# Attention with latent projections on one core: probabilities transposed and moved inside SBUF in one transfer, the division by the softmax sums put after the values, and two 64-row matmuls beside each other

## The chip, the cores and the metric

The kernel runs on one core of a Trainium2 chip. The metric is the device time of one execution in microseconds (us). Three executions of the kernel before took 1964.89, 1964.98 and 1975.46 us; the median is 1964.98 us.

Engines are named as the profile names them: PE is the matrix engine (PEld its weight loads), DVE the vector engine, ACT the scalar engine, POOL GpSimd, SP the engine that issues most DMAs. SBUF is the on-chip memory with 128 partitions, PSUM the matmul's result memory, DRAM the chip's large memory.

## The reference

```python
cq = rms_norm(x @ w_qa.T, q_a_ln_w)                       # x: 2048 x 512
q_nope, q_pe = split((cq @ w_qb.T), 128, 64)              # 16 heads
ckv = x @ w_kva.T                                         # 128 latent + 64 rotary columns
k_nope, v = split(rms_norm(ckv[..., :128], kv_a_ln_w) @ w_kvb.T)
scores = (q_nope @ k_nope.T + rope(q_pe) @ rope(k_pe).T) * 192 ** -0.5
attn = softmax(causal(scores))                            # 16 x 2048 x 2048
x = layernorm(x + (attn @ v) @ w_o.T)
x = layernorm(x + x @ (weight * scale_weight).T + bias)
```

The kernel keeps keys and values in the latent form of 128 columns (`w_kvb` is folded into the query weights and into `w_o`), so one set of keys `Kn`, `Kp` and values `V` serves all heads. Float32 accuracy is made of two parts: a number is stored as a rounded part and a rest, and a product is three matmuls (part by part, part by rest, rest by part).

## The kernel before

The 2048 queries are cut into four blocks b of 512, the 16 heads into eight pairs p. Within a block the loop `units` (L659) runs over the pairs, over four tiles qt of 128 queries, and over the two heads j of the pair. One such step, a **unit**, handles 128 queries of one head against nk = (4b + qt + 1) * 128 keys: 640 to 1024 keys in block 1, 1152 to 1536 in block 2, 1664 to 2048 in block 3. In block 0 (nk up to 512) both heads are one step. A unit has one PSUM tile of up to 1024 scores (two chunks of at most 512) where nk is at most 1024, and two tiles above.

A unit goes through these lines:

1. `score` (L421, matmuls at L431): for each chunk of keys five matmuls with 128 rows each: the query's latent part against both parts of `Kn`, its rest against the first, and two with `Kp`. In `pe`, rows 0 to 63 hold the rotary query's rounded part and rows 64 to 127 its rest; in `Kp`, rows 64 to 127 repeat rows 0 to 63. The first of the two products with `Kp` so adds (part + rest) by the key's part; the second adds (part + rest) by the key's rest.
2. DVE takes the maximum (L472) and makes the bias (L479 or L481); ACT takes the exponent into `pr` with the row's sum beside it (L487).
3. DVE makes `inv`, 16384 divided by the sum, in two small instructions (L497 or L499, and L500).
4. ACT writes `pr * inv` as float16 into the even halves of the 32-bit words of `hl` (L525), DVE the rest into the odd halves (L528).
5. `turn` (L503): DVE transposes the words in blocks of 32 x 32 (L506), back into `pr`, and SP sends the head's turned words to a DRAM tile `sq` (L509).
6. After the second head `gather` (L511) fetches both heads from `sq` into a slot of the SBUF tile `ring`, with four DMAs of 32 destination partitions each (L514). A DMA of SP waits in SP's queue, and all that is queued behind it waits too.
7. Two or three query tiles later `values` (L573, matmuls at L584) multiplies `V` with the slot. The result `ot` (L589) goes to `ot_d` in DRAM.

`pr` has 5, 3 and 2 buffers in blocks 1, 2 and 3, `hl` 4, 3 and 2; each holds a whole head. `room` (L739) gives out the slots of `ring` and runs values early where none is free. Projections of the next pair (L359, L403) are put between the units by `fill`. The order of PE and SP is as written in blocks 1 to 3, and that of DVE and ACT too from the second query tile of block 3; elsewhere a scheduler sets it.

After block 3 comes the **tail**: for 32 combinations of block and pair `latent_load` (L756) fetches `ot_d`, `latent_split` (L760) makes part and rest on ACT (L64) and DVE (L65), `accumulate` (L803) multiplies with the output weights; then the layer norms and the last matrix.

Of the kernel before, what the change touches and what calls it, by code (L numbers as in the profile page):

```python
# [49 lines left out]
def mla_block(ctx: ExitStack, tc: tile.TileContext, a, out):  # L50
# [23 lines left out]
    ot_d = [[dram.tile([P, 4, 256], F32, name=f"ot_d{b}_{p}") for p in range(NPAIR)] for b in range(NB)]  # L74

# [228 lines left out]
    later = []  # L304

# [41 lines left out]
    def project_pe(b, g, direct=None):  # L347
# [72 lines left out]

    def score(ps, c0, w, b, p, j, qt, masked):  # L421
# [14 lines left out]
        if by_product:  # L436
# [3 lines left out]
            mask()  # L440

# [3 lines left out]
    def head_scores(pools, b, p, j, qt, nk, prev):  # L445
# [6 lines left out]
        for ti, ck in enumerate(cks):  # L452
# [13 lines left out]
            for ci, (c0, w) in enumerate(ck):  # L466
# [17 lines left out]
        pr = pools[1].tile([P, nk], F32, tag="pr", name=f"pr{b}_{p}_{qt}_{j}", bufs=(5, 3, 2)[b - 1])  # L484
        sums = small.tile([P, 2], F32, tag="sums", name="sums")
        for ti, (v, c0, n, w) in enumerate(tiles):
            nc.scalar.activation(  # L487
                pr[:, c0 : c0 + n * w].rearrange("p (a c) -> p a c", a=n),
# [4 lines left out]
                accum_out=sums[:, ti : ti + 1],  # L493
            )
        inv = small.tile([P, 1], F32, tag="inv", name="inv")
        if nt == 1:
            nc.vector.tensor_scalar(inv, sums[:, 0:1], 1.0 / P_UP, None, ALU.mult)  # L497
        else:
            nc.vector.tensor_scalar(inv, sums[:, 0:1], sums[:, 1:2], 1.0 / P_UP, ALU.add, ALU.mult)  # L499
        nc.vector.reciprocal(inv, inv)  # L500
        return pr, inv

    def turn(words, sq, dst):  # L503


        nc.vector.transpose(  # L506
            sq.rearrange("p (k c r) -> p c k r", k=4, r=32), words.rearrange("p (c k r) -> p c k r", k=4, r=32)
        )
        nc.sync.dma_start(dst, sq.rearrange("p (k x) -> p k x", k=4))  # L509

    def gather(PT, src):  # L511

        for k in range(4):
            nc.sync.dma_start(  # L514
                PT[32 * k : 32 * k + 32].bitcast(F32).rearrange("p (q x) -> p q x", q=4),
                src[:, k].rearrange("(q p) x -> p q x", q=4),
            )

    def head_probs(pools, b, p, j, qt, nk, PT, pr, inv):
        words = pools[0].tile([P, nk], F32, tag="hl", name=f"hl{b}_{p}_{qt}_{j}", bufs=(4, 3, 2)[b - 1])  # L520
# [12 lines left out]
        sq = state["sq"]  # L533
        turn(words, pr, sq[:, :, j * nk // 4 : (j + 1) * nk // 4])
        if j == 1:
            gather(PT, sq)
        put_in()

    def pair_scores(pool, b, p, qt, nk):
# [11 lines left out]
        sums = small.tile([P, 2], F32, tag="sums", name="sums")  # L551
        for j in range(2):
            nc.scalar.activation(
                pr[:, j, :], ps[:, j, :nk], AF.Exp, bias=bias[:, j : j + 1], scale=r, accum_out=sums[:, j : j + 1]
            )
        inv = small.tile([P, 2], F32, tag="inv", name="inv")
        nc.vector.tensor_scalar(inv, sums, 1.0 / P_UP, None, ALU.mult)
        nc.vector.reciprocal(inv, inv)
        return pr, inv

    def pair_probs(pool, b, p, qt, nk, PT, pr, inv):
        words = pool.tile([P, 2 * nk], F32, tag=f"hl{qt}", name=f"hl{b}_{p}_{qt}")
        hl = words.bitcast(F16).rearrange("p (j n a) -> p j a n", j=2, a=2)
        for j in range(2):
            iv = inv[:, j : j + 1]
            nc.scalar.activation(hl[:, j, 0, :], pr[:, j, :], AF.Copy, scale=iv)
            nc.vector.scalar_tensor_tensor(hl[:, j, 1, :], pr[:, j, :], iv, hl[:, j, 0, :], ALU.mult, ALU.subtract)
        sq = dram.tile([P, 4, nk // 2], F32, tag="sq0", name=f"sq{b}_{p}_{qt}", bufs=4)
        turn(words, pr.rearrange("p j n -> p (j n)"), sq)
        gather(PT[:, : 4 * nk], sq)  # L570
        yield

    def values(b, p, qt, nk, PT):  # L573

        kts = nk // P
        v = PT[:, : 4 * nk].rearrange("p (q j k r a) -> p j a k q r", j=2, q=4, a=2, k=kts)
# [82 lines left out]
    def units(pool, ring, b):  # L659
        lag = min(ring.shape[1] // (2048 * (b + 1)) - 1, 3) if b else 2  # L660

        for p in range(NPAIR):
# [24 lines left out]
            for qt in range(4):  # L687
# [354 lines left out]
```

## Time and profile before

| | |
|---|---|
| median of three executions | 1964.98 us |
| the profiled execution | 1974.24 us, its span 1972.5 us |
| busy share of the span | PE 84%, DVE 73%, ACT 51%, POOL 17% |
| mean granted clock of PE | 0.936 |
| DMA traffic | 405.20 MB, 205 GB/s |
| HBM read, written | 225.77 MB, 177.73 MB |

The busy share is an average over stages. A wait is put down to the instruction or transfer that ended it. Matmul durations overlap, since matmuls are pipelined: the distance from start to start is shorter than the duration shown. The stages begin and end where DVE's first maximum of a block starts: start and block 0 to 285.7 us, block 1 to 609.2, block 2 to 1071.2, block 3 to 1696.5, then the tail.

### The profile page before, as it was taken

To read this page: it belongs to the slowest core of one execution; us is meant where nothing else is said; L and a number is where in the kernel's file an instruction comes from. 1 tells how busy PE (TensorE), PEld (TensorE's weight loads), DVE (VectorE), ACT (ScalarE), POOL (GpSimd) and SP (SyncE) were. 2 spreads that over 40 slices of the span, in tenths; PEclk is the share of its full clock that TensorE was granted. 3 is DMA by queue.
4 is the path that set the end of the run, shared out by engine and by line. 5 is a ranking of instruction groups with operands and counts; after the bars stand their busy time and mean duration, and the time that the engine had idled before them with its cause. 6 is when DMAs were issued, how large, how long until landed. Compare 5 with 4: busy or idle time off the path is not lost.

```text
span 1972.5 us, 25934 instructions
## 1 busy us (share of the span) xinstructions
PE 1661.1 (84%) x9292; PEld 1343.5 (68%) x9292; DVE 1442.4 (73%) x2200; ACT 998.9 (51%) x1633; POOL 334.1 (17%) x386
## 2 busy tenths in 40 slices
PE   8999778887888887888877878878887787699998
PEld 7778666666766676676665757656666566478876
DVE  6878668777777887788777867886887686645554
ACT  5767555555454565555555555554555555431220
POOL 2323323404034031040012400400400000001011
PEclk9999989988999999999989989998999898899999
DMA  7786656778787778887888777787777888853331
GB/s 241 247 269 210 214 161 194 205 210 227 206 228 210 222 204 228 224 224 211 221 247 240 204 223 200 213 219 214 201 224 193 243 218 241 216 179 112 118 118 38
DMA packets 248672, 405.20 MB, mean 205 GB/s; under 512 B 21952, under 2 KB 179008, under 8 KB 247520
## 3 DMA queue, kind: packets, MB, share of 16 engines
q1 hardware_dynamic: 236960, 376.11, 67.0%
q0 software_dynamic: 4672, 17.73, 2.9%
q10 hardware_dynamic: 6912, 9.70, 1.6%
q8 instruction: 74, 1.21, 0.3%
q14 instruction: 54, 0.44, 0.1%
HBM read 225.77 MB, written 177.73 MB: 205 GB/s over the span
## 4 chain that ended last, share of the span: by engine, by line
PE 20%; DMA 16%; DVE 13%; ACT 4%; issue 2%; SPq 1%; ACTq 0%; POOLq 0%; POOL 0%; DVEq 0%
DMA sq<-pr 11%; PE acc L803 8%; DVE hl L528 5%; DVE pr L506 4%; PE o L584 4%; DMA ring<-sq 4%; PE s L431 4%; DVE neg L472 3%; ACT pr L487 2%; PE ff L924 2%; ACT hl L525 2%; PE ps_qn L403 1%; SPq L514 1%; DMA o<-ot_d 0%; PE ps_wo L201 0%
## 5 line engine op out<-in xcount | busy, mean ns | idle before, releaser
L431 PE MATMUL s<-Kn,qn 128*128 128x512 f32 (+4 forms) x1920 | 533.8, 387 | 86.3 <-ACT pr L487 73.9
L584 PE MATMUL o<-ring,V 128*128 128x256 f16 x3024 | 407.1, 289 | 177.9 <-DMA ring<-sq 147.5
L584 PEld LDWEIGHTS <-V 128*128 128x128 f16 x3264 | 317.1, 101 | 293.9 <-issue 184.2
L487 ACT ACTIVATE pr<-s,bias,rq 128x1024 f32<-128x1024 f32 (+3 forms) x320 | 324.5, 1018 | 376.1 <-DMA sq<-pr 216.7
L431 PEld LDWEIGHTS s<-Kn,qn 128*128 128x128 f32 x1920 | 351.5, 199 | 149.4 <-ACT pr L487 91.6
L528 DVE SCALAR_TENSOR_TENSOR hl<-pr,inv,hl 128x1024 f16<-128x1024 f32 (+7 forms) x320 | 390.8, 1236 | 72.6 <-ACT hl L525 72.4
L525 ACT ACTIVATE hl<-pr,inv 128x1024 f16<-128x1024 f32 (+7 forms) x320 | 363.1, 1197 | 96.7 <-DVE inv L500 95.4
L472 DVE TENSOR_REDUCE neg<-s 128x1 f32<-128x1024 f32 (+3 forms) x320 | 314.6, 988 | 84.2 <-PE s L431 44.5
L431 PE MATMUL s<-Kp,pe 128*128 128x512 f32 (+4 forms) x1280 | 374.0, 374 | 0.0
L506 DVE STREAM_TRANSPOSE pr<-hl 128x256 f32<-128x256 f32 (+6 forms) x224 | 328.7, 1469 | 2.8
L431 PEld LDWEIGHTS s<-Kp,pe 128*128 128x128 f32 x1280 | 245.0, 198 | 31.8
L371 POOL TENSOR_TENSOR prod<-prod 128x512 f32<-128x512 f32 x15 | 19.3, 1288 | 905.6 <-DVE prod L364 905.6
L403 PE MATMUL ps_qn<-cq,wq 128*128 128x512 f32 x576 | 149.9, 406 | 1.6 <-ACT ot L589 0.9
L803 PE MATMUL acc<-wvo,oh 128*128 128x512 f32 x448 | 143.2, 400 | 1.5 <-ACT pr L487 1.5
L386 POOL TENSOR_TENSOR pe<-prod,ph 32x512 fp32r<-32x512 f32 x92 | 136.9, 1488 | 6.0
L589 ACT ACTIVATE ot<-o 128x256 f32<-128x256 f32 x128 | 48.7, 380 | 170.7 <-DMA ot_d<-ot 118.6
L403 PEld LDWEIGHTS ps_qn<-cq,wq 128*128 128x128 f32 x576 | 105.9, 193 | 21.9 <-ACT ot L589 1.2
L499 DVE TENSOR_SCALAR inv<-sums 128x1 f32<-128x1 f32 x128 | 25.2, 197 | 119.8 <-ACT pr L487 119.7
L803 PEld LDWEIGHTS acc<-wvo,oh 128*128 128x128 f32 x448 | 83.2, 188 | 22.1 <-issue 2.9
L803 PE MATMUL acc<-wvo,ol 128*128 128x512 f32 x224 | 88.0, 393 | 0.0
L359 PE MATMUL ps_pe<-cq,wpe 128*128 128x512 f32 x288 | 78.4, 420 | 6.2 <-DMA cq<-cq_d 4.6
L385 POOL CAST pe<-prod 32x512 fp32r<-32x512 f32 x88 | 67.1, 763 | 3.3
(156 smaller groups left out, 1619.7 us busy)
## 6 DMA issues: line engine op xcount, KB each, us to landing
wq<-wq_d SPq DMA_DIRECT2D x22, 768.0 KB, 8.1
sq<-pr SPq DMA_DIRECT2D x16, 1024.0 KB, 5.2
ring<-sq SPq DMA_DIRECT2D x32, 512.0 KB, 7.7
o<-ot_d SPq DMA_DIRECT2D x32, 512.0 KB, 3.5
sq<-pr SPq DMA_DIRECT2D x16, 960.0 KB, 6.0
ring<-sq SPq DMA_DIRECT2D x32, 480.0 KB, 8.3
sq<-pr SPq DMA_DIRECT2D x16, 896.0 KB, 4.4
ring<-sq SPq DMA_DIRECT2D x32, 448.0 KB, 7.1
```

The lines of the kernel that those rows point to most:

```text
L359: nc.tensor.matmul(ps, w[:, i, lt, x * P : (x + 1) * P], cq[:, k, lt, :], start=n == 0, stop=n == 8)
L385: nc.gpsimd.tensor_copy(to, rp[q, x, :])
L386: (nc.gpsimd if not quick or (b, g) == (0, 0) and j % 2 else nc.vector).tensor_tensor(pe[64 + 32 * x : 96 + 32 * x, j, :], rp[q, x, :], ph ...
L403: nc.tensor.matmul(ps, w[:, i, lt, j * P : (j + 1) * P], cq[:, k, lt, :], start=n == 0, stop=n == 8)
L431: nc.tensor.matmul(ps[:, :w], lhs, K[:, i, c0 : c0 + w], start=n == 0, stop=n == 4 and not by_product)
L472: nc.vector.tensor_reduce(neg[:, ti : ti + 1], v, axis=AX.XY, op=ALU.max, negate=True)
L487: nc.scalar.activation(pr[:, c0 : c0 + n * w].rearrange("p (a c) -> p a c", a=n), v, AF.Exp, bias=bias, scale=r, accum_out=sums[:, ti : ti ...
L506: nc.vector.transpose(sq.rearrange("p (k c r) -> p c k r", k=4, r=32), words.rearrange("p (c k r) -> p c k r", k=4, r=32))
L525: nc.scalar.activation(hl[:, 0, c], pr[:, c], AF.Copy, scale=inv)
L528: nc.vector.scalar_tensor_tensor(hl[:, 1, c], pr[:, c], inv, hl[:, 0, c], ALU.mult, ALU.subtract)
L584: nc.tensor.matmul(ps[:, :256], vt[:, i, k % 4, :], v[:, :, l, k, :], start=n == 0, stop=n == 3 * kts - 1)
L803: nc.tensor.matmul(acc, l[:, t, c], state["wvo"][p][:, i, j, :], start=p == 0 and j == 0 and n == 0, stop=p == NPAIR - 1 and j == 1 and n ...
```

## The change

The edits belong together:

- **One transfer in place of two.** `turn` reads the words of a chunk with a step of four words, so that after the transpose row r of a 32-row group holds the keys 4r to 4r + 3 of each chunk. Four DMAs, one for each group of 32 query rows, then go straight from `pr` to all 128 partitions of the `ring` slot. `sq` and `gather` are gone. `pr` and `hl` are now held by score tile and not by head: 5, 6, 5 and 4, 3, 3 buffers. The ring slot is chosen at the first turn of a query tile (`place`), and in block 3 values run half a query tile later.
- **The division is put off.** The probabilities are scaled by the constant 16384 alone. The sums of a pair's eight units lie in one tile; `settle` takes their reciprocals once for each pair during the next pair, and POOL's queue sends them to DRAM (`inv_d`), one word at a time. In the tail `latent_load` also fetches them, repeated over all partitions, and POOL multiplies `o` by them before the split.
- **Two 64-row matmuls.** Of the second product with `Kp`, the rest by rest is dropped. The remaining part by rest has 64 rows. For tiles with two chunks, `score_pair` issues it once on rows 0 to 63 (first chunk) and once on rows 64 to 127 (second chunk). For that, `pe` holds part and rest of the second two heads the other way round, and `other_half` copies the rounded parts to the other 64 partitions (`side`, two DMAs for four heads). It is left out for the first query tile of even pairs and for the last pair of block 3.

```diff
         for j in range(4):
             q = slice(32 * j, 32 * j + 32)
             for x in range(2):
-                to = pe[32 * x : 32 * x + 32, j, :]
+                at = 64 * (j // 2) + 32 * x
+                to = pe[at : at + 32, j, :]
+                at = 64 * (1 - j // 2) + 32 * x
                 if quick:
                     nc.scalar.activation(to, rp[q, x, :], AF.Copy)
                 else:
                     nc.gpsimd.tensor_copy(to, rp[q, x, :])
                 (nc.gpsimd if not quick or (b, g) == (0, 0) and j % 2 else nc.vector).tensor_tensor(
-                    pe[64 + 32 * x : 96 + 32 * x, j, :], rp[q, x, :], ph[q, x, :].bitcast(F32), ALU.subtract
+                    pe[at : at + 32, j, :], rp[q, x, :], ph[q, x, :].bitcast(F32), ALU.subtract
...
+    def other_half(b, g):
+        oh = state["side"] = state["prs"].tile([P, 2, QB], F32R, tag="side", name=f"side{b}_{g}")
+        pe = state["pe", b, g]
+        move(nc.sync, oh[64:128], pe[0:64, 0:2])
+        move(nc.sync, oh[0:64], pe[64:128, 2:4])
...
+    def score_pair(ps, ck, b, p, j, qt, nk):
...
+        qs = slice(qt * P, (qt + 1) * P)
+        qn = state["qn", b, p]
+        pe, side = state["pe", b, p // 2], state["side"]
+        qh, ql = qn[:, 0, j, qs], qn[:, 1, j, qs]
+        qp = pe[:, 2 * (p % 2) + j, qs]
+        for ci, (c0, w) in enumerate(ck):
+            for n, (lhs, K, i) in enumerate([(qh, Kn, 0), (qh, Kn, 1), (ql, Kn, 0), (qp, Kp, 0)]):
+                nc.tensor.matmul(ps[:, ci, :w], lhs, K[:, i, c0 : c0 + w], start=n == 0, stop=False)
+        sides = (qp, side[:, j, qs]) if p % 2 == 0 else (side[:, j, qs], qp)
+        for ci, (c0, w) in enumerate(ck):
+            half = slice(64 * ci, 64 * ci + 64)
+            d = nk - P - c0
+            masked = 0 <= d < w
+            nc.tensor.matmul(ps[:, ci, :w], sides[ci][half], Kp[half, 1, c0 : c0 + w], start=False, stop=not masked)
+        if masked:
+            nc.tensor.matmul(ps[:, 1, d : d + P], identb, maskb, start=False, stop=True)
...
+        if ("sums", b, p) not in state:
+            state["sums", b, p] = small.tile([P, 2 if b > 1 else 1, 8], F32, tag="sums", name=f"sums{b}_{p}", bufs=2)
+            due.append((b, p))
...
+        while due and due[0] != now:
+            b, p = due.pop(0)
+            sums = state.pop(("sums", b, p))
+            inv = small.tile([P, 8], F32, tag="inv", name=f"inv{b}_{p}", bufs=2)
+            if b > 1:
+                nc.vector.tensor_tensor(inv, sums[:, 0], sums[:, 1], ALU.add)
+                nc.vector.reciprocal(inv, inv)
+            else:
+                nc.vector.reciprocal(inv, sums[:, 0])
+            with nc.allow_non_contiguous_dma(reason="one word of each query"):
+                nc.gpsimd.dma_start(inv_d[b][p].rearrange("t q -> q t"), inv)
...
-            for ci, (c0, w) in enumerate(ck):
+            tiled = len(ck) == 2 and (p % 2 or qt) and (b, p) != (NB - 1, NPAIR - 1)
+            if tiled:
+                score_pair(ps, ck, b, p, j, qt, nk)
+            for ci, (c0, w) in enumerate(() if tiled else ck):
                 d = nk - P - c0
                 score(ps[:, ci, :], c0, w, b, p, j, qt, d if 0 <= d < w else None)
...
-        pr = pools[1].tile([P, nk], F32, tag="pr", name=f"pr{b}_{p}_{qt}_{j}", bufs=(5, 3, 2)[b - 1])
-        sums = small.tile([P, 2], F32, tag="sums", name="sums")
+        parts = []
         for ti, (v, c0, n, w) in enumerate(tiles):
+            pr = pools[1].tile([P, n * w], F32, tag="pr", name=f"pr{b}_{p}_{qt}_{j}_{ti}", bufs=(5, 6, 5)[b - 1])
             nc.scalar.activation(
-                pr[:, c0 : c0 + n * w].rearrange("p (a c) -> p a c", a=n),
+                pr.rearrange("p (a c) -> p a c", a=n),
...
-                accum_out=sums[:, ti : ti + 1],
+                accum_out=sums_of(b, p)[:, ti, 2 * qt + j : 2 * qt + j + 1],
             )
-        inv = small.tile([P, 1], F32, tag="inv", name="inv")
-        if nt == 1:
-            nc.vector.tensor_scalar(inv, sums[:, 0:1], 1.0 / P_UP, None, ALU.mult)
-        else:
-            nc.vector.tensor_scalar(inv, sums[:, 0:1], sums[:, 1:2], 1.0 / P_UP, ALU.add, ALU.mult)
-        nc.vector.reciprocal(inv, inv)
-        return pr, inv
-
-    def turn(words, sq, dst):
+            parts.append((pr, c0))
+        return parts
+    def turn(PT, x0, words, sq):
         nc.vector.transpose(
-            sq.rearrange("p (k c r) -> p c k r", k=4, r=32), words.rearrange("p (c k r) -> p c k r", k=4, r=32)
+            sq.rearrange("p (k c r) -> p k c r", k=4, r=32), words.rearrange("p (c r k) -> p k c r", k=4, r=32)
         )
-        nc.sync.dma_start(dst, sq.rearrange("p (k x) -> p k x", k=4))
-
-    def gather(PT, src):
-
-        for k in range(4):
-            nc.sync.dma_start(
-                PT[32 * k : 32 * k + 32].bitcast(F32).rearrange("p (q x) -> p q x", q=4),
-                src[:, k].rearrange("(q p) x -> p q x", q=4),
-            )
-
-    def head_probs(pools, b, p, j, qt, nk, PT, pr, inv):
-        words = pools[0].tile([P, nk], F32, tag="hl", name=f"hl{b}_{p}_{qt}_{j}", bufs=(4, 3, 2)[b - 1])
-        hl = words.bitcast(F16).rearrange("p (n a) -> p a n", a=2)
-        step = nk if nk <= 1024 else nk // 2
-        cuts = [slice(c, c + step) for c in range(0, nk, step)]
-        for c in cuts:
-            nc.scalar.activation(hl[:, 0, c], pr[:, c], AF.Copy, scale=inv)
+        n = sq.shape[1] // 4
+        to = PT.bitcast(F32).rearrange("p (q x) -> p q x", q=4)
+        for q in range(4):
+            rows = sq[32 * q : 32 * q + 32].rearrange("p (k x) -> p k x", k=4)
+            nc.sync.dma_start(to[:, q, x0 : x0 + n], rows)
+    def head_probs(pools, b, j, nk, PT, parts):
+        cut = []
+        for pr, c0 in parts:
+            words = pools[0].tile([P, pr.shape[1]], F32, tag="hl", name=f"hl{pr.name}", bufs=(4, 3, 3)[b - 1])
+            cut.append((pr, c0, words, words.bitcast(F16).rearrange("p (n a) -> p a n", a=2)))
+        for pr, c0, words, hl in cut:
+            nc.scalar.activation(hl[:, 0], pr, AF.Copy, scale=P_UP)
         yield
-        for c in cuts:
-            nc.vector.scalar_tensor_tensor(hl[:, 1, c], pr[:, c], inv, hl[:, 0, c], ALU.mult, ALU.subtract)
-            if c != cuts[-1]:
+        for n, (pr, c0, words, hl) in enumerate(cut):
+            nc.vector.scalar_tensor_tensor(hl[:, 1], pr, P_UP, hl[:, 0], ALU.mult, ALU.subtract)
+            if n + 1 < len(cut):
                 yield
-        if j == 0:
-            state["sq"] = dram.tile([P, 4, nk // 2], F32, tag=f"sq{b}", name=f"sq{b}_{p}_{qt}", bufs=4)
-        sq = state["sq"]
-        turn(words, pr, sq[:, :, j * nk // 4 : (j + 1) * nk // 4])
-        if j == 1:
-            gather(PT, sq)
+        for pr, c0, words, hl in cut:
+            turn(PT(), (j * nk + c0) // 4, words, pr)
         put_in()
...
-                    s0 = room(2048 * (b + 1), ring.shape[1], 4 * nk, (b, p) == (2, NPAIR - 1) and qt > 0)
-                    PT = ring[:, s0 : s0 + 4 * nk]
-                vg = values(b, p, qt, nk, PT)
+                    s0, PT = None, place(ring, 2048 * (b + 1), 4 * nk, (b, p) == (2, NPAIR - 1) and qt > 0)
...
                     for j in range(2):
+                        if 2 * qt + j == 1:
+                            settle((b, p))
+                            if p % 2 == 0:
+                                other_half(b, p // 2)
...
+                        run_values(lag + (b == 3 and j == 0))
...
+        if b == NB - 1:
+            settle()
...
+    def place(ring, n, need, dense):
+        entry = [None, 0, None, None]
+        def get():
+            if entry[2] is None:
+                s0 = room(n, ring.shape[1], need, dense)
+                entry[2:] = [s0, s0 + need]
+            return ring[:, entry[2] : entry[3]]
+        get.entry = entry
+        return get
...
     def latent_load(b, p, by=nc.sync.dma_start):
-        o = state["o", b, p] = state["pcr"].tile([P, 4, 256], F32, tag="o", name=f"o{b}_{p}")
+        o = state["pcr"].tile([P, 4, 256], F32, tag="o", name=f"o{b}_{p}")
         by(o, ot_d[b][p])
+        n, pool, tag = (4, state["pcr"], "iv") if b == 0 and p < 4 else (1, blk, "qn")
+        src = inv_d[b][p].rearrange("(n t) q -> n (t q)", n=n)
+        iv = [pool.tile([P, 1024 // n], F32, tag=tag, name=f"iv{b}_{p}_{i}", bufs=2) for i in range(n)]
+        for i in range(n):
+            by(iv[i], src[i].partition_broadcast(P))
+        state["o", b, p] = o, iv
...
-        split(state.pop(("o", b, p)), oh, ol)
+        o, iv = state.pop(("o", b, p))
+        parts = o.rearrange("p t q -> p (t q)").rearrange("p (n x) -> p n x", n=len(iv))
+        for i, v in enumerate(iv):
+            nc.gpsimd.tensor_tensor(parts[:, i], parts[:, i], v, ALU.mult)
+        split(o, oh, ol)
...
+    state["prs"] = ctx_p.enter_context(tc.tile_pool(name="prs", bufs=1, side="right", reuse_waits="tile"))
```

More of the change, by code (lines that the diff above doesn't have):

```diff
@@ L74, in mla_block @@
     ot_d = [[dram.tile([P, 4, 256], F32, name=f"ot_d{b}_{p}") for p in range(NPAIR)] for b in range(NB)]
+    inv_d = [[dram.tile([8, P], F32, name=f"inv_d{b}_{p}") for p in range(NPAIR)] for b in range(NB)]
     ident = const.tile([P, P], F32, name="ident")
@@ L304, in mla_block @@
     later = []
+    due = []
     def put_off(dst, src, n=0):
@@ L440, in score, with sums_of, settle @@
             mask()
+    def sums_of(b, p):
+        if ("sums", b, p) not in state:
+            state["sums", b, p] = small.tile([P, 2 if b > 1 else 1, 8], F32, tag="sums", name=f"sums{b}_{p}", bufs=2)
+            due.append((b, p))
+        return state["sums", b, p]
+    def settle(now=None):
+        while due and due[0] != now:
[9 more added lines that the diff above has]
+                nc.gpsimd.dma_start(inv_d[b][p].rearrange("t q -> q t"), inv)
     def head_scores(pools, b, p, j, qt, nk, prev):
@@ L550, in pair_scores, with pair_probs @@
         pr = pool.tile([P, 2, nk], F32, tag=f"pr{qt}", name=f"pr{b}_{p}_{qt}")
-        sums = small.tile([P, 2], F32, tag="sums", name="sums")
         for j in range(2):
             nc.scalar.activation(
-                pr[:, j, :], ps[:, j, :nk], AF.Exp, bias=bias[:, j : j + 1], scale=r, accum_out=sums[:, j : j + 1]
-            )
[L556 to L561, printed above, removed]
+                pr[:, j, :],
+                ps[:, j, :nk],
+                AF.Exp,
+                bias=bias[:, j : j + 1],
+                scale=r,
+                accum_out=sums_of(b, p)[:, 0, 2 * qt + j : 2 * qt + j + 1],
+            )
+        return pr
+    def pair_probs(pool, b, p, qt, nk, PT, pr):
         words = pool.tile([P, 2 * nk], F32, tag=f"hl{qt}", name=f"hl{b}_{p}_{qt}")
@@ L564, in pair_probs @@
         for j in range(2):
[L565 to L570, printed above, removed]
+            nc.scalar.activation(hl[:, j, 0, :], pr[:, j, :], AF.Copy, scale=P_UP)
+            nc.vector.scalar_tensor_tensor(
+                hl[:, j, 1, :], pr[:, j, :], P_UP, hl[:, j, 0, :], ALU.mult, ALU.subtract
+            )
+        turn(PT[:, : 4 * nk], 0, words, pr.rearrange("p j n -> p (j n)"))
         yield
@@ L575, in values @@
         kts = nk // P
-        v = PT[:, : 4 * nk].rearrange("p (q j k r a) -> p j a k q r", j=2, q=4, a=2, k=kts)
+        v = (PT() if b else PT)[:, : 4 * nk].rearrange("p (q j k r a) -> p j a k q r", j=2, q=4, a=2, k=kts)
         ps = psum["m"].tile([P, 512], F32, tag="m", name=f"o{b}_{p}_{qt}")
@@ L701, in units @@
                     flush()
-                    probs.append(pair_probs(pool, b, p, qt, nk, PT, *pi))
+                    probs.append(pair_probs(pool, b, p, qt, nk, PT, pi))
+                    if qt == 1:
+                        settle((b, p))
                     fill()
@@ L712, in units @@
                     for j in range(2):
+                        if 2 * qt + j == 1:
+                            settle((b, p))
+                            if p % 2 == 0:
+                                other_half(b, p // 2)
                         prepare_output(b, p, 2 * qt + j)
@@ L715, in units @@
                         pi = head_scores(pool, b, p, j, qt, nk, prev)
-                        probs.append(head_probs(pool, b, p, j, qt, nk, PT, *pi))
+                        probs.append(head_probs(pool, b, j, nk, PT, pi))
                         if (b, p, qt, j) == (1, 0, 1, 0):
@@ L721, in units @@
                             fill()
-                        run_values(lag)
-                vals.append([vg, 0, s0, s0 + 4 * nk])
+                        run_values(lag + (b == 3 and j == 0))
+                if b:
+                    tile_ = PT.entry
+                    tile_[0] = values(b, p, qt, nk, PT)
+                    vals.append(tile_)
+                else:
+                    vals.append([values(b, p, qt, nk, PT), 0, s0, s0 + 4 * nk])
             drain()
```

## The prediction

> **What bounds the kernel now.** I read the busy time by stage first. This answer gives, for each of the five stages that "Time and profile before" names, its length, then the busy time of PE, PEld, DVE, ACT and POOL with instruction counts, the granted clock, the DMA share and GB/s.
>
> ```profile
> 0.00:285.70 285.70, 242.30 (x1526) 208.06 (x1527) 208.80 (x466) 181.78 (x449) 83.31 (x154) 0.94 0.71 228
> 285.70:609.20 323.50, 268.29 (x1511) 219.66 (x1511) 242.42 (x416) 166.50 (x242) 81.00 (x72) 0.91 0.74 208
> 609.20:1071.20 462.00, 388.88 (x2227) 312.09 (x2225) 372.49 (x543) 260.69 (x434) 84.01 (x72) 0.96 0.81 223
> 1071.20:1696.50 625.30, 510.31 (x2897) 404.26 (x2895) 480.91 (x541) 331.90 (x435) 64.90 (x56) 0.92 0.79 216
> 1696.50:1972.50 276.00, 251.36 (x1139) 199.46 (x1137) 137.73 (x239) 58.08 (x73) 20.89 (x32) 0.96 0.40 125
> ```
>
> Blocks 1 to 3 take 1411 us. DVE is busy for 75%, 81% and 77% of them, the DMA engines for 74% to 81%. No engine is full; so I read the chain of waits in order of time (start, us, what), here two units of block 3:
>
> ```profile
> 1287.66 11.25 DMA sq<-pr
> 1299.02 2.49 ACT pr L487 x4
> ...
> 1315.70 2.31 DVE pr L506
> 1318.04 4.42 DMA sq<-pr
> ...
> 1323.91 10.98 DMA ring<-sq
> 1335.03 4.19 PE o L584 x24
> ```
>
> The exponent waits 11 us until a `pr` buffer has been written to DRAM; the values then wait for the way out (4.4 us), the queue and the way back (11.0 us). With two `pr` buffers for the exponent, the casts, the turn and the write, block 3 goes at the pace of these latencies. The list of waits (engine, line, releaser: us in total, times, longest) has the same names at its head:
>
> ```profile
> ACT pr L487 <- DMA sq<-pr: 216.7, 58, 12.0
> ...
> PE o L584 <- DMA ring<-sq: 147.5, 41, 8.8
> DVE inv L499 <- ACT pr L487: 119.7, 43, 10.0
> ```
>
> So three things bind together: the two-hop latency, DVE, which is next, and PE close behind.
>
> **DVE, step by step.** The groups by form give the prices (count, busy us, mean ns):
>
> ```profile
> L506 DVE STREAM_TRANSPOSE pr<-hl 128x2048 f32<-128x2048 f32 x16 | 37.0, 2312 | 0.6
> L506 DVE STREAM_TRANSPOSE pr<-hl 128x256 f32<-128x256 f32 x8 | 3.5, 436 | 0.0
> L499 DVE TENSOR_SCALAR inv<-sums 128x1 f32<-128x1 f32 x128 | 25.2, 197 | 119.8 <-ACT pr L487 119.7
> L497 DVE TENSOR_SCALAR inv<-sums 128x1 f32<-128x1 f32 x64 | 9.2, 144 | 26.0 <-ACT pr L487 26.0
> L500 DVE RECIPROCAL inv<-inv 128x1 f32<-128x1 f32 x192 | 29.7, 155 | 3.3
> ```
>
> - Gone: `inv`. Block 1 has 64 units at 144 + 155 ns, 19.1 us; blocks 2 and 3 have 64 each at 197 + 155 ns, 22.5 us each; block 0 loses 32 steps at 168 + 162 ns (L557, L558), 10.6 us. The stops ahead of L499 and L497 (119.7 and 26.0 us) go as well, in part: DVE then waits for ACT's casts instead.
> - Added: a transpose costs (2312 - 436) / 1792 = 1.047 ns a word and 168 ns once. Blocks 2 and 3 turn two tiles instead of one head: 64 x 168 ns = 10.8 us each. `settle`: 8 times 155 ns in blocks 0 and 1, 8 times some 350 ns in blocks 2 and 3: 1.2 and 2.8 us.
> - Sum: block 0 199.4 us, block 1 224.5, block 2 363.6, block 3 472.0.
> - Unknown: the transpose now reads with a step of four words. No row here reads so. Lower end: no change, 1.047 ns (a gain is excluded: the words are the same, and a long transpose already runs at a constant price for each). Upper end: the dearest word of any elementwise group, POOL's L371 with 1288 / 512 = 2.5 ns. I take 1.047, the row of the same operation on the same engine; a second pass over each word would be 2.09.
>
> The Trainium skill speaks against this step. The page "SBUF — State Buffer" ("Door 1: The DMA port swizzle") says that SBUF has lines of 16 bytes, that full bandwidth needs two hits in a line, and that each access to another line is penalized; the new read hits every line once. It gives no size for the penalty; a price twice as high would give the second rival's sum below.
>
> **DMA.** The turned words are 20480 + 53248 + 86016 + 118784 = 278528 for each of 128 partitions, 142.6 MB; they moved twice, 285 of 405 MB. Now they move once; `iv` adds 32 x 0.5 MB and `side` 24 x 0.25 MB, about 286 MB in all. The latency from turn to ring falls from 4.4 + 1.4 + 11.0 us to four issues of 0.43 us and one landing (5.2 us is the median of the 1 MB write). The two waits on `sq` and `ring` should all but vanish: a `pr` tile is then held for some 10 us, and five tiles serve 2.5 units of over 8 us. SP issues 740 DMAs more (1736 for 996); in block 3 that is 8 x 0.43 = 3.4 us of a unit's 9.8, which delays the `wq` loads behind them by no more. `put_in` keeps its place. The ring slot is asked for one unit earlier; in block 3 the values that free it have been issued ahead of the scores of the same unit.
>
> **PE.** Five matmuls of 512 columns follow each other at 1.17 us, 0.234 each:
>
> ```profile
> 1305.90 0.63 PE L431 MATMUL s<-Kp,pe 128*128 128x512 f32 x2
> 1306.37 0.86 PE L431 MATMUL s<-Kn,qn 128*128 128x512 f32 x3
> 1307.07 0.63 PE L431 MATMUL s<-Kp,pe 128*128 128x512 f32 x2
> ```
>
> 208 tiles get the 64-row pair: 126 of 512 columns, 30 of 448, 38 of 384, 14 of 320. If the two run fully beside each other, one distance each is saved (231, 200, 174, 146 ns): 43.7 us. No 64-row matmul stands in the trace. The other end: before and after each pair the matmul in flight has to finish first; a 512-column matmul is shown with 398 ns at a distance of 231, so 208 x 2 x 0.167 = 69 us are added, and 26 us lost in the net. I take the saving, but count neither end: PE's start-to-start sums in blocks 1 to 3 are 240, 356 and 465 us, 74% to 77%, so DVE covers it. Without that cover it would be worth up to 44 us.
>
> The page "TensorEngine Tiling (Array Packing)" ("Key Properties") states that changing the tiling mode drains TensorE; by it the second end would be the nearer one, and it would still lie under DVE's time.
>
> **The rest.** `side` lands (3.5 us for 256 KB, as `x`) before the second query tile, a unit of 5 us or more later: nothing. ACT keeps its 384 casts: nothing. POOL issues 32 small DMAs at 0.57 us (L309) beside its 334 us: nothing. In the tail POOL multiplies 1024 words per pair, 2.6 to 3.0 us by L371 and L372 (1288 and 1492 ns for 512). An `o` buffer is held for 3.5 (landing) + 3.0 + 1.1 (L64) + 1.2 (L65) = 8.8 us; with two, 4.4 us per pair, under PE's 24 x 0.227 = 5.4 us, so PE covers it. If the doubled loads land 2 us later, up to 1 us for each of 32 pairs shows: 0 to +32 us, taken as +5.
>
> **The sum.** With the two-hop waits gone, I let DVE reach in all three blocks the share that block 2 has already, 372.49 / 462 = 80.6%; there the `sq` wait counts least for its length.
>
> - block 1: 224.5 / 0.806 = 278.5, -45.0 us
> - block 2: 363.6 / 0.806 = 451.1, -10.9
> - block 3: 472.0 / 0.806 = 585.6, -39.7
> - block 0: -5, of the 12.9 that 9.4 us of DVE are at its share of 73%
> - tail: +5
>
> Together -96 us: the profiled execution's 1974.24 would be 1878. That execution lies 9 us above the median shown, 1964.98; from the median it is **1869 us**. With the best slice's share (83.5%, 700 to 800 us) the three blocks would give -141 and block 0 -13: the lower end, 1810.
>
> **Rivals.**
>
> 1. The waits come back as others. For: the list also has ACT waiting for the bias (75.4 us), PE for PSUM tiles that the exponent frees (73.9), DVE for the casts (72.4). Against: the chain of block 3 is half DMA. DVE's shares stay as they are: 224.5 / 0.749, 363.6 / 0.806, 472.0 / 0.769 give -23.8, -10.9, -11.5; with block 0 and the tail -46: 1919; with the tail at +32, 1946.
> 2. The turn's step of four words makes DVE the bound, in L506's successor. At 2.09 ns, blocks 1 to 3 get 55.7, 90.1 and 124.4 us more; at 90% busy (PE reaches 91% in the tail, where it alone binds) they take 311, 504 and 663 us, +67; with block 0 at 0 and the tail +5, **2037 us**. It decides from (0.9 x 1411 - 1060) / 258 + 1.047 = 1.86 ns a word. Against: writes of `hl` in half words (L528, 1434 ns for 1024) cost little more than L65's whole words (1222). For: nothing in the trace excludes it. At 2.5 ns it would be 2150.
> 3. The 64-row matmuls do not run beside each other: then PE loses up to 26 us, hidden as above. It changes no sign.
>
> **How the numbers follow.** Forecast 0.55 (1810 to 1905), first rival 0.20, second 0.25. 1% is about what a measurement of this kernel can tell from no change. Faster by more than 1%: 0.55 and 0.14 of the first rival, 0.69; within 1%: 0.07; slower: 0.24. The range 1810 to 2040 leaves out 0.04 below and some 0.12 above, the dearer half of the second rival.
>
> **What would show it.** Right: no wait of ACT's exponent or of the values on a DMA among the longest; DVE 80% or more in blocks 1 to 3; transposes of 1024 words near 1.24 us; two 64-row matmuls a few ns apart; DMA traffic near 286 MB; in the tail PE at 91% as now. Wrong: transposes above 1.9 us for 1024 words, DVE at 90% and PE's share falling; or POOL's product ahead of ACT's L64 in the tail's waits.

## The result, and the profile after

The changed kernel takes 1982.88 us (median of 12 executions, 1965.54 to 1990.18), the kernel before in the same sessions 1964.93 us (12 executions, 1958.62 to 1975.46): a ratio of **1.0082, 95% interval 1.0055 to 1.0110**. It is slower by 0.8%, where 1869 us had been forecast. The profiled execution took 1983.77 us, its span is 1982.0 us.

The busy time by stage, as shown of before: length, then PE, PEld, DVE, ACT and POOL with instruction counts, clock, DMA share and GB/s. The stages are again cut where DVE's first maximum of a block starts.

```profile
0.00:299.20 299.20, 246.53 (x1534) 209.97 (x1534) 210.88 (x410) 174.52 (x448) 89.73 (x161) 0.91 0.74 184
299.20:627.20 328.00, 266.90 (x1497) 203.63 (x1498) 264.45 (x296) 165.43 (x243) 88.87 (x81) 0.91 0.65 135
627.20:1097.60 470.40, 400.53 (x2245) 299.07 (x2243) 415.24 (x498) 253.61 (x436) 91.01 (x80) 0.93 0.61 133
1097.60:1674.00 576.40, 501.33 (x2861) 374.32 (x2860) 532.79 (x487) 311.77 (x433) 76.40 (x69) 0.95 0.61 135
1674.00:1982.00 308.00, 260.54 (x1158) 204.72 (x1158) 147.99 (x242) 57.91 (x73) 93.73 (x71) 0.94 0.48 151
```

Against before the stages are +13.5, +4.5, +8.4, -48.9 and +32.0 us. DVE has *more* work in blocks 1 to 3: 1212.5 us for 1095.8, though `inv` is gone. Its share is 81%, 88% and 92%. DMA moves 285.96 MB for 405.20. In the tail POOL is busy 93.7 us for 20.9.

The work that DVE gained stands in the groups by form (count, busy us, mean ns, idle time before):

```profile
L559 DVE STREAM_TRANSPOSE pr<-hlpr 128x1024 f32<-128x1024 f32 x144 | 289.0, 2018 | 0.0
L578 DVE SCALAR_TENSOR_TENSOR hlpr<-pr,hlpr 128x1024 f16<-128x1024 f32 x144 | 202.3, 1406 | 44.0 <-ACT hlpr L575 44.0
...
L559 DVE STREAM_TRANSPOSE pr<-hlpr 128x768 f32<-128x768 f32 x48 | 74.3, 1548 | 0.2
```

The transpose has become DVE's dearest group. From 768 to 1024 words it grows by (2018 - 1548) / 256 = 1.84 ns a word; before it was 1.047.

The list of waits (engine, line, releaser: us in total, times, longest):

```profile
ACT pr L544 <- DVE bias L538: 105.2, 34, 9.1
ACT pr L544 <- DVE bias L536: 101.4, 33, 13.2
POOL o L846 <- DMA o<-ot_d: 96.0, 19, 11.8
...
ACT pr L544 <- DMA ring<-pr: 91.5, 25, 13.3
DVE hlpr L578 <- ACT hlpr L575: 90.9, 50, 7.4
PE s L450 <- DMA side<-pe: 90.3, 10, 14.3
```

Of the two waits on the hops, that of PE's values on `ring` (147.5 us) is down to 1.0 us; that of ACT's exponent on the transfer out of its `pr` buffer (216.7 us) is down to 91.5 us. The exponent now waits longer in total for DVE (the bias stands behind the long transposes), and PE waits for `side`, nine times for 7 to 14 us and once briefly, in nearly every even pair. The chain that ended last reaches back only into the tail in this profile, so the timeline stands in its place: one of these waits in order of time (start, us, engine, line), with lines of PE, DVE and SP only:

```profile
541.76 2.00 DVE L559 STREAM_TRANSPOSE pr<-hlpr 128x1024 f32<-128x1024 f32 x1
...
543.84 2.73 SPq L566 DMA_DIRECT2D ring<-pr  x4
545.15 2.48 DVE L559 STREAM_TRANSPOSE pr<-hlpr 128x640 f32<-128x640 f32 x2
549.88 1.78 SPq L59 DMA_DIRECT2D side<-pe  x2
551.76 5.99 SPq L566 DMA_DIRECT2D ring<-pr  x8
...
554.71 0.69 PE L450 MATMUL s<-Kp,side 64*128 64x384 f32 x1 [14.33 <-DMA side<-pe]
```

SP takes its DMAs in order. The four `ring` DMAs stand behind a transpose, `side` behind them; it is issued at 549.9 us and lands at 554.7. `pe` had been written at 481.0 us. During the wait DVE runs out of scores too. SP's own list says where its time goes:

```profile
SPq L566 <- DVE pr L559: 386.2, 142, 11.1
...
SPq L566 <- DMA ring<-pr: 39.6, 17, 5.8
```

The second row is a limit that I had not seen. The DMAs of SP take turns on eight semaphores, and each waits until the eighth before it has landed. The `side` DMA above waited for this from 546.6 us on: the eighth before it, issued at 540.2, landed at 549.8. Right ahead of `side` SP stood still in only two of PE's ten waits, for 4.5 and 3.3 us; in the other eight `side` followed the DMA before it within 0.2 us, so there it came late because the `ring` DMAs ahead of it had, or because of its own landing. Of the 90.3 us, 51 had passed when SP had issued `side`, and 40 came after that. The landings of its 24 DMAs spread widely:

```profile
DMA to landing us min/median/max: 2.9/4.4/9.5
```

PE's timeline shows the 64-row pair itself:

```profile
1410.63 0.39 PE L444 MATMUL s<-Kp,pe 128*128 128x512 f32 x1
1410.95 0.50 PE L450 MATMUL s<-Kp,pe 64*128 64x512 f32 x1
1410.96 0.50 PE L450 MATMUL s<-Kp,side 64*128 64x512 f32 x1
1411.39 0.79 PE L444 MATMUL s<-Kn,qn 128*128 128x384 f32 x3
```

The two do run beside each other: the second starts 3 ns after the first (median of 126 pairs of 512 columns). But the step from the full matmul to the pair takes 318 ns and the step to the next full one 428 ns, for 231 between two full ones. A pair costs 318 + 3 + 428 = 749 ns, two full matmuls 3 x 231 = 693.

### The profile page after: what moved, and what is told of

The parts are those of the page before. It is cut to its first block, busy times and chain, and to the rows that moved or that the text cites. A ratio compares the mean times of both kernels' runs of the same rounds, so it can differ in the third digit from the quotient of the medians.

```text
span 1982.0 us, 27732 instructions
## 1 busy us (share of the span) xinstructions
PE 1675.8 (85%) x9292; PEld 1291.7 (65%) x9292; DVE 1571.3 (79%) x1928; ACT 963.2 (49%) x1633; POOL 439.7 (22%) x462
## 2 busy tenths in 40 slices
DMA packets 281006, 285.96 MB, mean 144 GB/s; under 512 B 59392, under 2 KB 254336, under 8 KB 279840
## 5 line engine op out<-in xcount | busy, mean ns | idle before, releaser
L559 DVE STREAM_TRANSPOSE pr<-hlpr 128x1024 f32<-128x1024 f32 (+3 forms) x320 | 509.4, 1619 | 0.4
L578 DVE SCALAR_TENSOR_TENSOR hlpr<-pr,hlpr 128x1024 f16<-128x1024 f32 (+3 forms) x320 | 367.1, 1159 | 91.1 <-ACT hlpr L575 90.9
L444 PE MATMUL s<-Kn,qn 128*128 128x512 f32 (+3 forms) x1248 | 357.7, 396 | 36.5 <-ACT pr L544 36.2
L575 ACT ACTIVATE hlpr<-pr 128x1024 f16<-128x1024 f32 (+3 forms) x320 | 341.8, 1113 | 20.3 <-DVE pr L559 14.8
L464 PE MATMUL s<-Kn,qn 128*128 128x512 f32 (+3 forms) x672 | 174.2, 367 | 48.3 <-ACT pr L544 38.2
L450 PE MATMUL s<-Kp,side 64*128 64x512 f32 (+3 forms) x208 | 103.4, 497 | 90.3 <-DMA side<-pe 90.3
L444 PE MATMUL s<-Kp,pe 128*128 128x512 f32 (+3 forms) x416 | 157.6, 379 | 0.0
L450 PEld LDWEIGHTS s<-Kp,side 64*128 64x128 f32 x208 | 39.6, 191 | 128.6 <-DMA side<-pe 93.3
L846 POOL TENSOR_TENSOR o<-o,iv 128x1024 f32<-128x1024 f32 (+1 forms) x44 | 80.5, 1834 | 182.7 <-DMA o<-ot_d 96.0
L464 PE MATMUL s<-Kp,pe 128*128 128x384 f32 (+3 forms) x448 | 119.7, 349 | 0.0
L450 PE MATMUL s<-Kp,pe 64*128 64x512 f32 (+3 forms) x208 | 100.9, 485 | 0.0
```

The source lines that it names most:

```text
L444: nc.tensor.matmul(ps[:, ci, :w], lhs, K[:, i, c0 : c0 + w], start=n == 0, stop=False)
L450: nc.tensor.matmul(ps[:, ci, :w], sides[ci][half], Kp[half, 1, c0 : c0 + w], start=False, stop=not masked)
L464: nc.tensor.matmul(ps[:, :w], lhs, K[:, i, c0 : c0 + w], start=n == 0, stop=n == 4 and not by_product)
L559: nc.vector.transpose(sq.rearrange("p (k c r) -> p k c r", k=4, r=32), words.rearrange("p (c r k) -> p k c r", k=4, r=32))
L575: nc.scalar.activation(hl[:, 0], pr, AF.Copy, scale=P_UP)
L578: nc.vector.scalar_tensor_tensor(hl[:, 1], pr, P_UP, hl[:, 0], ALU.mult, ALU.subtract)
```

## The experiments

Ratios are against the kernel before, run in the same session. It took 1958.98, 1961.75, 1965.93 and 1963.77 us in the four sessions, so a difference in us between kernels of different sessions can be off by some 7 us. By the ratios, the 101, 89 and 54 us that follow are 93, 81 and 51, and the 28 us that the pairs cost where PE binds are 22.

**What a step costs.** In the kernel before, the transpose of pair 0 is left as runs of words, and the pairs 1 to 7 each read or write `pr` and `hl` with another step. Its output leaves out the right order of the words.

```diff
-        nc.vector.transpose(
-            sq.rearrange("p (k c r) -> p c k r", k=4, r=32), words.rearrange("p (c k r) -> p c k r", k=4, r=32))
+        if p == 0:
+            nc.vector.transpose(runs(sq, 4), runs(words, 4))
+        if p == 1:
+            nc.vector.transpose(runs(sq, 2), by(words, 2))
...
+        if p == 7:
+            nc.vector.transpose(by(sq, 8), runs(words, 8))
```

> The kernel before with another step of the transpose in each of the eight pairs, the words so going to wrong places: pair 0 reads and writes runs, pairs 1 to 4 read with a step of 2, 4, 8 and 32 words, pairs 5 to 7 write with a step of 2, 4 and 8. By the lines it gives the price of 1024 words: runs 1.24 us. If the price is a second access for each line of 16 bytes, step 2 costs as runs do and steps 4, 8 and 32 all 2.0 us; if it grows with the step, each is dearer than the one before. For the writes nothing is known; cheap or dear, it tells if the step could have stood on the other side.

The kernel was run once (2005.76 us); what counts is its groups for 1024 words. L513 has no step; L515, L517, L519 and L521 read with steps of 2, 4, 8 and 32 words, L523, L525 and L527 write with 2, 4 and 8:

```profile
L519 DVE STREAM_TRANSPOSE pr<-hl 128x1024 f32<-128x1024 f32 x3 | 6.5, 2173 | 0.0
...
L527 DVE STREAM_TRANSPOSE pr<-hl 128x1024 f32<-128x1024 f32 x3 | 6.4, 2132 | 0.0
...
L525 DVE STREAM_TRANSPOSE pr<-hl 128x1024 f32<-128x1024 f32 x3 | 6.0, 2010 | 0.0
L517 DVE STREAM_TRANSPOSE pr<-hl 128x1024 f32<-128x1024 f32 x3 | 6.0, 2007 | 0.0
...
L521 DVE STREAM_TRANSPOSE pr<-hl 128x1024 f32<-128x1024 f32 x3 | 5.8, 1921 | 0.0
...
L513 DVE STREAM_TRANSPOSE pr<-hl 128x1024 f32<-128x1024 f32 x3 | 3.8, 1267 | 0.0
...
L515 DVE STREAM_TRANSPOSE pr<-hl 128x1024 f32<-128x1024 f32 x3 | 3.7, 1232 | 0.0
L523 DVE STREAM_TRANSPOSE pr<-hl 128x1024 f32<-128x1024 f32 x3 | 3.7, 1229 | 0.0
```

A step of 8 bytes costs nothing. Steps of 16 and 32 bytes, read or written, and of 128 bytes, read, take 1921 to 2173 ns for some 1240. It is a threshold between 8 and 16 bytes, not a slope. That fits the rule of the Trainium skill that the prediction cited against the step ("SBUF — State Buffer", "Door 1: The DMA port swizzle"): two words in a line of 16 bytes are enough, one is not. The price is here 0.67 to 0.91 ns a word, 0.75 for the step of 16 bytes.

**The step alone**, put into the kernel before (keys meet rows of `V` that aren't theirs; the work is the same):

```diff
-            sq.rearrange("p (k c r) -> p c k r", k=4, r=32), words.rearrange("p (c k r) -> p c k r", k=4, r=32)
+            sq.rearrange("p (k c r) -> p c k r", k=4, r=32), words.rearrange("p (c r k) -> p c k r", k=4, r=32)
```

> The kernel before with one edit: the transpose reads with a step of four words; keys so meet the wrong rows of V, which changes no time. Theory S: 1024 words take 2.0 us for 1.24, DVE is busy about 200 us more in blocks 1 to 3, and the kernel is 60 to 130 us slower than before (2025 to 2095). Rival W: DVE has the slack (23% idle), and it is less than 20 us slower.

Measured: 2037.76 us (2034.82 to 2044.74), ratio 1.0407 (1.0371 to 1.0442): 79 us slower with nothing else changed.

**The step undone** in the changed kernel: the transpose reads runs again, and the inputs are laid out so that the keys still come to their rows of `V` (`project_x` puts the columns of queries and keys back into order in its splits, which the lines here leave out).

```diff
-            sq.rearrange("p (k c r) -> p k c r", k=4, r=32), words.rearrange("p (c r k) -> p k c r", k=4, r=32)
+            sq.rearrange("p (k c r) -> p k c r", k=4, r=32), words.rearrange("p (c k r) -> p k c r", k=4, r=32)
...
-    d["xT"] = x.T.reshape(KT, P, 2 * NB, 256).transpose(2, 1, 0, 3)
+    d["xT"] = x.T.reshape(KT, P, 2 * NB, 2, 4, 32).transpose(2, 1, 0, 3, 5, 4).reshape(2 * NB, P, KT, 256)
```

> The changed kernel, but the transpose reads runs of 32 words again (the rows of V stand in another order instead, so the result is the same). Theory S, the step of four words made DVE the bound: a transpose of 1024 words goes from 2.02 us back to about 1.24, DVE is busy some 200 us less in blocks 1 to 3 (1212 to about 1010 us), and the time falls by 110 to 190 us, to 1790 to 1870. Rival W, PE's waits for the side tile (90 us) and the tail (308 us for 276) are what eats the gain: the time falls by less than 40 us, and the waits for side stay near 90 us.

Measured: 1881.58 us (1878.12 to 1890.47), ratio 0.9611 (0.9575 to 0.9648). The step cost the change 101 us, a little less than the 110 to 190 expected. The group is back at its old price, and what is left in PE's waits is `side`:

```profile
L565 DVE STREAM_TRANSPOSE pr<-hlpr 128x1024 f32<-128x1024 f32 x144 | 176.6, 1236 | 0.0
```

```profile
PE s L456 <- DMA side<-pe: 77.5, 10, 14.6
```

**The 64-row products undone**, with the step kept: all tiles take `score`, and `other_half` isn't called.

```diff
-            tiled = len(ck) == 2 and (p % 2 or qt) and (b, p) != (NB - 1, NPAIR - 1)
+            tiled = False
...
-                            if p % 2 == 0:
-                                other_half(b, p // 2)
```

> The changed kernel without the 64-row matmuls: every second product with Kp uses 128 rows, and the side tile and its DMAs are gone. Theory S: DVE binds, and PE's 90 us of waiting for side are time in which it had run ahead of DVE; the time stays within 20 us of the changed kernel. Rival W: the waits for side are lost time; without them, and with 44 us of PE more, 40 to 90 us are gained.

Measured: 1893.57 us (1887.08 to 1898.55), ratio 0.9669 (0.9627 to 0.9711), 89 us less than the changed kernel. With either part alone the change would have been a gain of 3% to 4%; together they turn it into a loss. Which half of this part costs, the pair or its `side`?

**The pair without `side`:** both 64-row matmuls take their weights from `pe`.

```diff
-        sides = (qp, side[:, j, qs]) if p % 2 == 0 else (side[:, j, qs], qp)
+        sides = (qp, qp)
...
-                            if p % 2 == 0:
-                                other_half(b, p // 2)
```

> The changed kernel with its pairs of 64-row matmuls, but both read their weights from pe, so the side tile and its two DMAs are gone; one of the two products meets the wrong half of the words, which is what the kernel leaves out. If the wait for side is what the 64-row pair costs (90.3 us in 10 waits in the changed kernel), the time falls to some 1893 to 1920 us. If it is the change of the array's shape (about 87 ns before and 197 ns behind a pair), the time stays at 1965 us or more.

Measured: 1896.07 us (1890.16 to 1899.86), ratio 0.9665 (0.9621 to 0.9709), not to be told from the kernel with full rows. The 89 us are those of `side`; the pair's own price is covered while DVE binds.

**`side` issued earlier.** First with SP, one head earlier in the written order; then from POOL's queue too, which is the last pair of lines here (and the same for the other half).

```diff
+                        if p % 2 == 0 and 2 * qt + j == 0:
+                            other_half(b, p // 2)
                         if 2 * qt + j == 1:
                             settle((b, p))
-                            if p % 2 == 0:
-                                other_half(b, p // 2)
...
-        move(nc.sync, oh[64:128], pe[0:64, 0:2])
+        move(nc.gpsimd, oh[64:128], pe[0:64, 0:2])
```

> The changed kernel with the two DMAs of side still in SP's queue, but one head earlier in the written order (at the start of each even pair). The kernel that also moved them to POOL's queue lost its waits on side and took 1917.5 us. If the place in the order is what counts, this one loses them too and comes to within 15 us of 1917.5. If SP's queue is what counts, since every DMA there stands behind ring DMAs that wait for DVE, some of the waits stay and the time lies between 1930 and 1983 us.

> The changed kernel, with the two DMAs of side issued one head earlier (at the start of each even pair) and from POOL's queue instead of SP's, where they stand behind the ring DMAs that wait for DVE's turn. If the wait for side comes from that place in SP's queue, the waits of PE on side (90.3 us) fall under 20 us and the time comes to that of the kernel without side, 1896.1, within 15 us. If it is the one buffer or the landing itself, the waits stay and the time is above 1950 us.

Measured: with SP 1929.27 us (1921.90 to 1930.19), ratio 0.9821 (0.9784 to 0.9859), and five waits of PE are left:

```profile
PE s L450 <- DMA side<-pe: 29.7, 5, 11.1
```

With POOL 1917.47 us (1909.24 to 1926.27), ratio 0.9772 (0.9741 to 0.9804), and PE waits for `side` no more. Most of the loss was the place in the order: one head gives 54 us back, and the time is within 15 us of the other kernel's, as expected if the place counts. But the waits do not all go. In four of the five, SP had issued `side` before PE came to it, and PE waited for the landing, which took 4 to 11 us from the issue. POOL's queue issues `side` earlier (the first of these at 361.2 us, SP at 369.7), and these waits go too. Without waits the kernel stays 21 us above the one that has no `side` at all, above the 15 us that I had allowed; what the 24 transfers still cost there I can't say.

**Both parts undone:**

> Both parts undone at once: the transpose reads runs of words (the order of the keys is turned in the layout instead), and every rotary product uses all rows of the array, without the side tile. What stays of the change is the one hop and the product with the reciprocals behind the values. If the two costs are separate, their gains add: 1982.9 - 101.3 - 89.3 = 1792 us. If PE is next once DVE has its old price (PE busy 1137 us in blocks 1 to 3 with full rows, at the 91% that it reaches in the last stage 1249 us, 126 us less than the changed kernel takes there), some 1850 us. In both cases below either part alone (1881.6 and 1893.6).

Measured: 1827.85 us (1824.89 to 1828.26), ratio **0.9319 (0.9288 to 0.9351)**. The two gains do not add (1792); the sum falls between the two expectations. The stages:

```profile
0.00:291.80 291.80, 243.53 (x1533) 208.56 (x1534) 196.44 (x410) 174.31 (x449) 89.64 (x162) 0.93 0.75 187
291.80:571.20 279.40, 254.06 (x1499) 207.54 (x1498) 224.07 (x296) 163.88 (x242) 88.20 (x80) 0.96 0.73 152
571.20:992.60 421.40, 379.80 (x2236) 308.99 (x2235) 353.31 (x497) 259.09 (x436) 91.45 (x80) 0.96 0.68 143
992.60:1521.80 529.20, 483.15 (x2872) 391.85 (x2870) 449.08 (x488) 313.10 (x433) 81.65 (x69) 0.97 0.67 144
1521.80:1825.30 303.50, 262.53 (x1160) 206.33 (x1158) 143.72 (x242) 57.98 (x73) 93.58 (x71) 0.93 0.47 154
```

PE is now the fullest engine, 90% to 91% of blocks 1 to 3, DVE at 80% to 85%. This is the one hop and the delayed division by themselves: 134 us less than before.

**The tail.** First the product and its loads are left out of the changed kernel; then, in the kernel with both parts undone, DVE makes the product of the tail's pairs in POOL's place.

```diff
-            nc.gpsimd.tensor_tensor(parts[:, i], parts[:, i], v, ALU.mult)
+            eng = nc.vector if state["queue"] is nc.gpsimd else nc.gpsimd
+            eng.tensor_tensor(parts[:, i], parts[:, i], v, ALU.mult)
```

> The changed kernel without the loads of the reciprocals and without POOL's product with them; the output leaves out the division by the sums. The last stage took 308 us against 276 before. If the product and its loads are what it lost, it comes back to 276 to 285 us and the whole to 1950 to 1960 us. If the last stage lost the time to something else (the values left over at its start, the loads of o), it stays within 10 us of 308.

> Both parts undone, and in the last stage the product with the reciprocals runs on DVE (busy 148 of 308 us there) instead of POOL (94). If POOL's product is in the way there, 15 to 30 us below the kernel with both parts undone; if it is the landing of o and of the reciprocals, within 8 us of it.

Without the product 1935.82 us (1933.50 to 1942.77), ratio 0.9879 (0.9841 to 0.9917). The last stage is 284.2 us, so 24 of the 32 us lost there are the product with its loads. (Block 0 is 13 us shorter in that profile too, and blocks 1 to 3 together 12, so the whole lies below the 1950 to 1960 us expected. Blocks 0 of kernels that hardly differ there took 286 to 301 us; this spread isn't explained.) With DVE's product 1819.22 us (1815.73 to 1831.29), ratio 0.9290 (0.9244 to 0.9335), and a last stage of 298.1 us for 303.5. The 5 us of the stage, and the 8.6 us of the whole, which the intervals do not tell from nothing, are nearer to what was expected if the landing counts (within 8 us) than to POOL's product (15 to 30). DVE's wait is the one that POOL had:

```profile
DVE o L851 <- DMA o<-ot_d: 60.8, 23, 8.4
```

In the tail `o` now shares the queue with 0.5 MB of repeated reciprocals for each pair, and lands 4.5 us after its issue for 3.5 before (medians). That the doubled loads are the cause of what is left was not separated from the longer hold of `o`.

**The pair where PE binds:** the natural read and DVE's product with the 64-row pairs, `side` early from POOL. It differs from the last kernel in the pairs and in `side`.

> The natural read and DVE's product in the last stage as in the kernel that took 1819.2 us, but with the 64-row pairs, and side issued early from POOL. With DVE at its old price PE is busy 91% of block 3, so a pair should tell now: if two parallel 64-row matmuls save a distance each, up to 43.7 us less, some 1780 us; if a pair costs as much as it saves (in the changed kernel 749 ns for two products of 512 columns against 693 for two with full rows, 16 us over 208 pairs), 1815 to 1840 us.

Measured: 1847.30 us (1839.67 to 1855.81), ratio 0.9402 (0.9362 to 0.9441): 28 us *more* than with full rows (22 by the ratios) and above both expectations, though no wait for `side` is left. PE's busy time in blocks 1 to 3, first with pairs:

```profile
299.00:587.70 288.70, 264.54 (x1505) 201.63 (x1504) 225.23 (x296) 164.38 (x243) 93.95 (x89) 0.95 0.73 155
587.70:1016.40 428.70, 391.33 (x2239) 297.78 (x2238) 352.17 (x498) 257.66 (x436) 94.09 (x88) 0.95 0.70 145
1016.40:1548.90 532.50, 495.27 (x2869) 372.02 (x2867) 452.03 (x487) 312.25 (x433) 82.00 (x75) 0.97 0.67 146
```

then with full rows:

```profile
301.10:581.90 280.80, 252.89 (x1499) 206.52 (x1498) 223.94 (x296) 164.12 (x242) 88.20 (x80) 0.96 0.73 151
581.90:1001.90 420.00, 381.13 (x2236) 310.07 (x2235) 353.57 (x498) 257.98 (x436) 91.40 (x80) 0.96 0.68 143
1001.90:1531.40 529.50, 487.23 (x2871) 395.69 (x2870) 449.53 (x488) 312.72 (x433) 80.55 (x69) 0.96 0.67 143
```

Pairs take 11.7, 10.2 and 8.0 us more of PE, and the blocks are 7.9, 8.7 and 3.0 us longer. From the starts, 208 pairs cost 126 x 56 + 30 x 95 + 38 x 107 + 14 x 147 ns = 16 us of PE net (the last three for 448, 384 and 320 columns, read as for 512). What is left of the 28 or 22 us isn't settled: the last stage, in which no pair runs, took 303.9 us for 298.1, and the early `side` is one candidate. POOL stands still for 349 us there, in nine waits of up to 52.5, until PE has let go of the one `side` buffer; but the waits of other engines for POOL do not grow (the longest in blocks 1 to 3, ACT's for `prod`, is 9.8 us in total for 10.4), so this is not shown to cost anything.

**One buffer more.** The 4 KB that `side` left free go to `pr`.

```diff
-            pr = pools[1].tile([P, n * w], F32, tag="pr", name=f"pr{b}_{p}_{qt}_{j}_{ti}", bufs=(5, 6, 5)[b - 1])
+            pr = pools[1].tile([P, n * w], F32, tag="pr", name=f"pr{b}_{p}_{qt}_{j}_{ti}", bufs=(6, 7, 5)[b - 1])
```

> The kernel with both parts undone and DVE's product (1819.2 us), with one pr buffer more in blocks 1 and 2 (6 and 7 for 5 and 6), in the 4 KB that side left free. In that kernel the exponent waits 107.4 us on ring DMAs that still read pr. If these waits bind in blocks 1 and 2, 5 to 15 us less; if DVE and PE (84% and 91% busy in block 2) bind, no difference within 6 us.

Measured: 1816.67 us (1810.51 to 1818.57), ratio **0.9245 (0.9205 to 0.9286)**. That is 2.6 us under the kernel with one buffer less, whose executions overlap with these: no difference that was shown. Still, with the natural read, full rows and DVE's product it is 7.5% faster than before.

## Why the prediction was wrong

- **The step that failed first is the transpose's price.** I took "1.047, the row of the same operation on the same engine" between ends of 1.047 and 2.5 ns. Measured were 1.82 to 1.84, which is (1.83 - 1.047) x 258048 words = 202 us more of DVE in blocks 1 to 3; with the step undone DVE's busy time there fell by 186 us, from 1212.5 to 1026.5. The row that I called nearest had the same operation, but not the access pattern that the edit changed; only the words of `hl` (halves of words, 4-byte step) stood near it, and they are far below the threshold. The second rival named the mechanism, and the point from which it decides (1.86 ns) lies beside the price measured. That its 2037 us are also what the step alone makes of the kernel before (2037.76) is a coincidence, since they were worked out for 2.09 ns a word and with the hop gone. The changed kernel came out lower; its DVE sums, 415 and 533 us in blocks 2 and 3, lie below what that rival had (454 and 596).
- **"`side` lands before the second query tile: nothing"** failed by 90 us of waits on PE. I worked out the landing (3.5 us; 4.4 measured), not the queue in front of it: four `ring` DMAs for each turn, which wait for DVE. That is the greater part, 51 of the 90 us. The rest is the landing, which was not always near its median: in the three waits of block 3 it took 7 to 10 us from the issue, and why stays open. I had written that a DMA of SP holds up all behind it, and applied it to `wq` only.
- **PE's pair** lay inside its bounds (43.7 us saved or 26 lost): 16 us lost by the starts. The stated cover was right too: with DVE binding it costs nothing (1896.07 against 1893.57), without that cover the kernel with pairs is 28 us slower (22 by the ratios). The pair's parallel run was right, the third rival wrong, and the saving still isn't there, since the steps into and out of the pair take it back.
- **The tail's product** was put at +5 within 0 to +32: +32, of which 24 go with it. DVE's taking it over gave 5 us there, with 60.8 us of waits for `o` left on DVE; what the other 8 of the 32 us are stays open.
- **SP's issues** took 0.602 us (median), not 0.43, and the limit of eight DMAs under way had no place in the sum.
- **Right:** the values' wait on `ring` vanished with the hop. The exponent's wait on a transfer did not: at 91.5 us, with a longest of 13.3, it is still among the longest, which the signs for the forecast had excluded. DMA traffic came to 286.0 MB for 286 forecast. Block 3 took 576 us for 586, but by luck: with a DVE at 92% of a larger sum instead of 80.6%. With both mis-priced steps out of the way the forecast's blocks are 278.5, 451.1 and 585.6 us against 279.4, 421.4 and 529.2 measured: DVE's share rises further than the 80.6% that I let it reach (80%, 84%, 85%), and its sums were 10 and 23 us smaller than mine in blocks 2 and 3. The plan was worth more than forecast, 134 us and not 96; two of its details cost it all.

## What to carry to other kernels

When a change alters how an operation walks through memory, take its price from a row with that walk, not from a row with the same name; where no row has it, ask for the point from which the price decides, and let a nearby threshold weigh in the chances. A small transfer is priced by the queue that issues it: list what is ahead of it in order and what each of those waits for, and allow for a landing well above the median. And two half-height matmuls that truly run together are only a gain if the steps into and out of them cost less than the matmul that they save; put them next to each other in numbers before counting it.

## What the runs showed of the hardware that I had not expected

- A DVE transpose of 4-byte words costs the same with a step of 8 bytes as with none (1229 to 1267 ns for 1024 words), and 1.55 to 1.75 times as much with steps of 16 and 32 bytes, read or written, and of 128 bytes, read.
- Two 64-row matmuls on the two halves of the array start 3 ns apart; for 512 columns the step from a full-height matmul is 318 ns and the step back 428 ns, for 231 otherwise (medians in the changed kernel).
- In the changed kernel no SP DMA was issued before the eighth one ahead of it had landed (862 of them, those whose eighth has a landing in the trace); it is the program's eight semaphores that set this. Where four are issued for each turn, this reaches back two turns (39.6 us of SP's time in 17 waits).
